# Half of the states of a selective scan form their input on ScalarE and TensorE, and the sum over states is made of transposes

## The chip, the cores and the metric

The kernel runs on one core of a Trainium2 chip. The metric is the device time of one execution in microseconds (us), the median of a few runs. Five engines work at once, each through its own queue in order: TensorE (PE, with its weight loads as PEld), VectorE (DVE), ScalarE (ACT), GpSimd (POOL) and SyncE (SP, which here only issues DMAs).

## The reference

Two layers are computed. The change touches the first, a two-dimensional selective scan over a (4, 48, 48, 128) input. Each image is normalised, projected to 256 channels, convolved with a depthwise 3x3 filter and passed through SiLU. The 48x48 positions are then read in four orders (by rows, by columns, and both backwards), and in each order a recurrence with 16 states per channel runs over all 2304 positions:

```
def step(h, inp):
    dt_l, u_l, B_l, C_l = inp
    dA = jnp.exp(dt_l[..., None] * A)
    h = h * dA + (dt_l * u_l)[..., None] * B_l[:, :, None, :]
    y = jnp.einsum('bkdn,bkn->bkd', h, C_l)
```

B and C are one number per position and state, dt and u one per position and channel, A one per channel and state. The four results are added, with the term D*u, then normalised over the channels, gated with a SiLU branch and projected to 128 channels. The second layer, a spectral attention block, is the same before and after the change.

## The kernel before

Channels lie on the 128 partitions, in two halves (NF = 2), and positions along the free axis. An image's direction is cut into chunks of 480, 480, 480, 480 and 384 positions. The order of the work is written out by hand: for each image, direction and chunk, the 16 states are 16 *steps*, 1280 in all. `advance` puts a new step into a window of ten and runs the stages of the table `LAGS` on the steps in it, each stage a fixed number of steps behind:

- `fetch`: SP reads the rows of C for two states from DRAM, spread over all partitions (`cbc`); for every fourth state also the row of B (`bbc`).
- `spread`: for the other states TensorE makes the row of B on all partitions, a bf16 matmul with the selecting matrix `pick`, into the one PSUM buffer `pb`.
- `drive_in`: VectorE multiplies `du` (dt*u) with that row into `db`, 128x960; `drive_pool` does it on GpSimd for every fourth state, from `bbc`.
- `decay`: ScalarE makes exp(dt*A) for the two halves in `da`, one of two PSUM buffers, and copies the value carried from the chunk before into the element of `db` between the halves.
- `scan`: VectorE runs the recurrence h = da*h + db over both halves in one instruction. Between the halves da is 0, so that the second half starts from its own carried value.
- `read_out`: GpSimd multiplies h with the row of C (`hc`). `carry_on`: ScalarE copies the last value of each half into `carry`.
- `sum_up`: TensorE adds `hc` to the PSUM accumulators `yp` by a matmul with the identity, one per half. The first step of a chunk also adds D*u or the sum of the earlier directions (`y`).
- `put_away`: after the last state ScalarE copies `yp` out, into `y`, or in the last direction into `yb`, from which the generator `back` finishes the chunk.

At the end of each `advance`, `piece` takes one piece of the side work that waits in `later`: generators that project the next direction (`project`, `project_chunk`), prepare the next image (`front`) or finish chunks (`back`). They use the PSUM bank `pp`. `drive` makes `du` for the next chunk on GpSimd. All engine instructions but the DMAs are kept in the order in which they are written; nearly all bear the line number of that wrapper (L50), so that the profile's groups are told apart by the tiles' names.

Of the kernel before, what the change touches and what calls it, by code (L numbers as in the profile page):

```python
# [21 lines left out]
L = T * H  # L22
D = 256
NF = D // 128
N = 16
# [6 lines left out]
LC = 480  # L32
CHUNKS = [(s, min(LC, L - s)) for s in range(0, L, LC)]
# [20 lines left out]
def first_layer(ctx, tc, io, x1_dram, sp_dram, d_w, d_m):  # L54
# [16 lines left out]
    ring = ctx.enter_context(tc.tile_pool(name="l0_ring", bufs=7))  # L71
# [3 lines left out]
    ps_y = ctx.enter_context(tc.tile_pool(name="l0_psy", bufs=1, space=PSUM))  # L75
    dram = ctx.enter_context(tc.tile_pool(name="l0_dram", bufs=8, space=DRAM))
# [25 lines left out]
    w_x = const.tile([128, K, NF, R + 2 * N], F32, name="w_x")  # L102
# [6 lines left out]
    p3 = const.tile([NX, N], F32, name="p3")  # L109
# [63 lines left out]
    def open_up(b, x, made):  # L173
# [3 lines left out]
        st = small.tile([128, 6, 6], F32, tag="st", name=f"st{b}")  # L177
# [180 lines left out]

    def load_dt(b, k):
        w_dt = two.tile([32 + R, D], F32, tag="w_dt", name=f"w_dt{b}_{k}")  # L360
        nc.sync.dma_start(w_dt[32 : 32 + R], io["dt_proj_wT"][k])
        return w_dt

    def project_chunk(c, w_dt, xc):
# [10 lines left out]
        xd = two.tile([32 + R, LC], F32, tag="xd", name=f"xd{c.t}")  # L375
# [12 lines left out]
        for f in range(NF):  # L388
            pd = side(f"pd{c.t}_{f}")
            on.tensor.matmul(  # L390
                pd[:, 0:n],
                w_dt[32 : 32 + R, f * 128 : (f + 1) * 128],
                xd[32 : 32 + R, 0:n],
                start=True,
                stop=True,
            )
            yield
            on.scalar.activation(c.dt[:, f, 0:n], pd[:, 0:n], AF.Identity, bias=b_dt[:, k, f : f + 1])

# [74 lines left out]
    NQ = 2  # L474

    das = [ps_a.tile([128, 2 * BANK], F32, name=f"da{j}") for j in range(2)]
    for da in das:
        on.vector.memset(da[:, BANK - 1 : BANK], 0.0)  # L480
    carries = [const.tile([128, N, NF], F32, name=f"carry{j}") for j in range(2)]

    def halves(ap, n):

        return ap[:, 0 : 2 * (n + 1)].rearrange("p (f n) -> p f n", f=NF)[:, :, 0:n]
# [10 lines left out]
    class Step:  # L496


        def __init__(self, c, i):
            self.c, self.i = c, i  # L500

    def fetch(u):
        c, i, n = u.c, u.i, u.c.n
        if i % NQ == 0:
            c.cbc = three.tile([128, NQ, LC], F32, tag="cbc", name=f"cbc{c.t}_{i}")
            nc.sync.dma_start(c.cbc[:, :, 0:n], c.cd[N + i : N + i + NQ, 0:n].partition_broadcast(128))
        u.cbc = c.cbc[:, i % NQ : i % NQ + 1, 0:n]
        if i % 4 == POOLS:
            u.bbc = two.tile([128, 1, LC], F32, tag="bbc", name=f"bbc{c.t}_{i}")
            nc.sync.dma_start(u.bbc[:, :, 0:n], c.cd[i : i + 1, 0:n].partition_broadcast(128))  # L510

    def drive_pool(u):

        c, i, n = u.c, u.i, u.c.n
        u.db = three.tile([128, NF * (LC + 1)], F32, tag="db", name=f"db{c.t}_{i}")
        if i % 4 == POOLS:
            on.gpsimd.tensor_mul(halves(u.db, n), c.du[:, :, 0:n], u.bbc[:, :, 0:n].to_broadcast([128, NF, n]))

    def spread(u):
# [4 lines left out]
        if i % 4 == POOLS:  # L524
# [4 lines left out]
        )  # L529

    def drive_in(u):
        c, i, n = u.c, u.i, u.c.n
        if i % 4 != POOLS:
# [4 lines left out]
    def decay(u):  # L538
        c, i, n = u.c, u.i, u.c.n
        u.da = das[i % 2]  # L540
        for f in range(NF):
            q = c.k * NF + f
            o = BANK if f else BANK - 1 - n
            on.scalar.activation(u.da[:, o : o + n], c.dt[:, f, 0:n], AF.Exp, scale=a_neg[:, q, i : i + 1])
        on.scalar.copy(u.db[:, n : n + 1], c.carry[:, i, 1 - c.rev : 2 - c.rev])

    def scan(u):
        c, i, n = u.c, u.i, u.c.n
        u.h = four.tile([128, NF * (LC + 1)], F32, tag="h", name=f"h{c.t}_{i}")
        m = 2 * n + 1  # L550
        ha, aa, ba = u.h[:, 0:m], u.da[:, BANK - 1 - n : BANK + n], u.db[:, 0:m]
# [4 lines left out]
    def read_out(u):  # L556
        c, i, n = u.c, u.i, u.c.n
        u.hc = four.tile([128, NF, LC], F32, tag="hc", name=f"hc{c.t}_{i}")
        on.gpsimd.tensor_mul(u.hc[:, :, 0:n], halves(u.h, n), u.cbc.to_broadcast([128, NF, n]))

    def carry_on(u):
        c = u.c
        if not c.final:
            on.scalar.copy(c.carry[:, u.i], halves(u.h, c.n)[:, :, 0 if c.rev else c.n - 1])

    def sum_up(u):

        c, i, n = u.c, u.i, u.c.n
        if i == 0:
            c.yp = [ps_y.tile([128, 512], F32, tag=f"yp{f}", name=f"yp{c.t}_{f}") for f in range(NF)]  # L570
            for f in range(NF):
                if c.k == 0:
                    on.tensor.matmul(
                        c.yp[f][:, 0:n], ddiag[:, f], c.im["xc"][:, f, c.s : c.s + n], start=True, stop=False
                    )
                else:
                    yv = at(c.im["y"], c.k, c.s, n)[:, f]
                    on.tensor.matmul(like(c.yp[f][:, 0:n], c.k), ident, yv, start=True, stop=False)
        for f in range(NF):
            on.tensor.matmul(c.yp[f][:, 0:n], ident, u.hc[:, f, 0:n], start=False, stop=(i == N - 1))  # L580

    def put_away(u):
# [4 lines left out]
        if c.k == ORDER[-1]:  # L587
            while len(backs) > 1:
                drain(backs.popleft())
            yb = two.tile([128, NF, LC], F32, tag="yb", name=f"yb{c.t}")  # L590
            for f in range(NF):
                on.scalar.copy(yb[:, f, 0:n], c.yp[f][:, 0:n])
            backs.append(back(c.b, c.s, n, yb, c.im["x"], c.im["w"], c.im["wb"]))
            later.append(backs[-1])
        else:
            if "y" not in c.im:
# [1390 lines left out]
```

## Time and profile before

| | us |
|---|---|
| median of 3 runs | 4990.82 |
| lowest and highest | 4985.44, 4992.6 |
| the profiled execution, span | 4987.4 |
| first scan begins, last scan ends | 76.8, 4178.2 |

The profiled execution is known by its span alone: no time of its own was taken outside it. The median of the runs, which are other executions, is 3.4 us above it. In the lines of the profile, a group of instructions is told by line, engine, operation, output<-inputs, shapes and count; then its busy time in us and the mean of one in ns; then the idle time of the engine just before it and what ended that. An f32 matmul is recorded as two, each with its weight load; a transpose as one. "128*96 128x128" on a matmul means weights of 128x96 and a moving operand of 128x128.

### The profile page before, as it was taken

Reading aid. Unit: us, or ns where it says so; the run is one execution under the profiler, and the core shown is the slowest. Engines: PE = TensorE matmul, PEld = TensorE weight load, DVE = VectorE, ACT = ScalarE, POOL = GpSimd, SP = SyncE. Lnnn points to the kernel's source line nnn. Section 1 sums busy time; section 2 is a strip of 40 time slices with the busy share of each in tenths; the row PEclk is TensorE's granted clock in tenths of the full one; section 3 lists DMA queues with packets and bytes.
Section 4 is the critical chain, followed back from the end, with each engine's and each line's share of the span. In section 5 each row is a group of like instructions: output and inputs, shape, how many; then the busy total and the mean of one; then the engine's idle time right before and its main releaser. Section 6 shows DMA issues by size and latency. Waiting matters only on the chain.

```text
span 4987.4 us, 44228 instructions
## 1 busy us (share of the span) xinstructions
PE 4176.6 (84%) x12444; PEld 1913.7 (38%) x12444; DVE 4169.9 (84%) x2901; ACT 2964.0 (59%) x6608; POOL 3992.7 (80%) x2188
## 2 busy tenths in 40 slices
PE   6888898888798998887989888877888786879876
PEld 3334433333343333333433333333333432445443
DVE  3599998989899989898999998888999985557636
ACT  3566566666666666766666676665767654323344
POOL 4589998989899989888999998888999985146631
PEclk9989999999899999998999999998999988989977
DMA  1223232323232333232323233233333322236636
GB/s 55 74 87 100 94 113 91 104 85 102 90 107 94 116 95 99 89 100 92 104 95 115 93 98 94 98 104 92 104 107 102 105 92 90 48 71 147 146 101 151
DMA packets 276388, 491.57 MB, mean 99 GB/s; under 512 B 105685, under 2 KB 189781, under 8 KB 275565
## 3 DMA queue, kind: packets, MB, share of 16 engines
q1 hardware_dynamic: 270560, 485.67, 32.5%
q10 hardware_dynamic: 5580, 3.08, 0.3%
q8 instruction: 98, 1.61, 0.1%
q14 instruction: 150, 1.22, 0.1%
HBM read 453.49 MB, written 35.38 MB: 98 GB/s over the span
## 4 chain that ended last, share of the span: by engine, by line
DVE 18%; PE 15%; issue 7%; ACT 7%; POOL 3%; DMA 2%; SPq 1%; DVEq 0%; POOLq 0%; ACTq 0%
DVE h L50 12%; PE yp L50 4%; ACT da L50 3%; DVE db L50 3%; PE acc L1404 2%; ACT L50 1%; PE sc L1267 1%; POOL v L1400 1%; POOL db L50 1%; PE pi_p L50 1%; DMA xrep<-dxt 1%; ACT dt L50 1%; POOL hc L50 1%; ACT ws L50 1%; PE px L50 1%
## 5 line engine op out<-in xcount | busy, mean ns | idle before, releaser
L50 POOL TENSOR_TENSOR hc<-h,cbc 128x960 f32<-128x960 f32 (+1 forms) x1280 | 2718.7, 2140 | 448.3 <-DVE h L50 335.8
L50 DVE TENSOR_TENSOR_SCAN h<-da,carry,db 128x961 f32<-128x961 f32 (+1 forms) x1280 | 2701.8, 2129 | 164.9 <-ACT carry L50 107.1
L50 ACT ACTIVATE da<-dt,a_neg 128x480 f32<-128x480 f32 (+1 forms) x2560 | 1666.6, 651 | 1176.6 <-DVE h L50 1130.8
L50 PE MATMUL yp<-hc,ident 128*128 128x480 f32 (+1 forms) x5120 | 2277.5, 572 | 17.7 <-POOL hc L50 17.4
L50 PEld LDWEIGHTS yp<-hc,ident 128*128 128x128 f32 x5120 | 1005.6, 198 | 1381.0 <-issue 1006.0
L50 DVE TENSOR_TENSOR db<-du,pb 128x960 f32<-128x960 f32 (+1 forms) x960 | 1063.8, 1108 | 233.2 <-PE pb L50 177.8
L50 POOL TENSOR_TENSOR db<-du,bbc 128x960 f32<-128x960 f32 (+1 forms) x320 | 688.9, 2153 | 17.2 <-DMA d_m<-in_wK 8.5
L50 PE MATMUL pb<-bs,pick 112*128 112x480 bf16 (+1 forms) x960 | 358.0, 373 | 351.9 <-DVE db L50 350.0
L50 PE MATMUL pc<-pad,cdiag 128*128 128x480 f32 (+1 forms) x630 | 284.1, 563 | 6.6 <-ACT pad L50 6.6
L1400 POOL TENSOR_TENSOR v<-grep,xrep 128x768 f32<-128x768 f32 x96 | 174.9, 1823 | 87.3 <-PE acc L1404 48.7
L50 ACT COPY db<-carry 128x1 f32<-128x1 f32 x1280 | 228.5, 178 | 19.5 <-POOL db L50 13.5
L1404 PE MATMUL acc<-v,attn_c 128*64 128x384 f32 x1152 | 211.5, 504 | 26.7 <-DVE v L1396 13.6
L50 POOL TENSOR_TENSOR du<-dt,xc 128x480 f32<-128x480 f32 (+1 forms) x160 | 204.9, 1281 | 34.0 <-ACT dt L50 34.0
L1396 DVE TENSOR_TENSOR v<-gp,xrep 128x1536 f32<-128x1536 f32 x96 | 168.0, 1756 | 74.4 <-PE acc L1404 46.4
L50 PE MATMUL px<-xc,w_xp 128*112 128x480 f32 (+1 forms) x320 | 214.0, 756 | 17.1 <-ACT xc L50 13.3
L50 PEld LDWEIGHTS <-pick 112*128 112x128 bf16 x960 | 97.7, 102 | 329.4 <-issue 306.1
L50 ACT ACT_TABLE_LOAD x148 | 189.9, 1283 | 50.3 <-DMA ws_M<-in_wM1s 26.7
L50 PE MATMUL pd<-xd,w_dt 8*128 8x480 f32 (+1 forms) x320 | 168.0, 605 | 40.0 <-ACT bs L50 24.5
L50 ACT COPY carry<-h 128x2 f32<-128x2 f32 x1024 | 194.4, 190 | 0.0
L50 PEld LDWEIGHTS pc<-pad,cdiag 128*128 128x128 f32 x630 | 122.1, 194 | 139.4 <-issue 114.6
L50 PE MATMUL yp<-y,ident 128*128 128x480 f32 (+1 forms) x240 | 166.3, 823 | 0.2
L1404 PEld LDWEIGHTS acc<-v,attn_c 128*64 128x64 f32 x1152 | 119.2, 139 | 108.5 <-issue 53.7
(366 smaller groups left out, 3102.2 us busy)
## 6 DMA issues: line engine op xcount, KB each, us to landing
cbc<-cd SPq DMA_DIRECT2D x512, 480.0 KB
bbc<-cd SPq DMA_DIRECT2D x256, 240.0 KB
cbc<-cd SPq DMA_DIRECT2D x128, 384.0 KB
xrep<-dxt SPq DMA_DIRECT2D x48, 576.0 KB
bbc<-cd SPq DMA_DIRECT2D x64, 192.0 KB
grep<-dgt SPq DMA_DIRECT2D x16, 576.0 KB
x<-in_xT SPq DMA_DIRECT2D x16, 288.0 KB
xr<-in_xT SPq DMA_DIRECT2D x16, 288.0 KB
```

The lines of the kernel that those rows point to most:

```text
L50: return lambda *args, **kw: self._tc.keep_in_program_order(emit(*args, **kw))
L1267: nc.tensor.matmul(sc[64 * b : 64 * b + 64, g, 0 : 8 * T], qs[:, j, n, 2 * pair + b], f[b][:, 8 * g : 8 * g + 8], start=(jn == 0), stop=False,
L1396: nc.vector.tensor_mul(v, gp[:, None, :, 0:NC].to_broadcast([128, 2, 2, NC]), x[:, :, 0:2])
L1400: nc.gpsimd.tensor_mul(v3, r[:, 2:3].to_broadcast([128, 2, NC]), x[:, :, 2])
L1404: nc.tensor.matmul(acc[c][64 * b : 64 * b + 64, 0:NC], attn_c[:, 2 * pair + b, g, q], v[:, b, c] if c < 2 else v3[:, b], start=first, stop ...
```

## The change

States with an even number keep the way through `pb` and VectorE; none is made on GpSimd any more. States with an odd number go another way. For each chunk `turn_du` transposes `du` on TensorE, so that positions lie on partitions, in blocks of 128 (`blocks`), and ScalarE copies it out of PSUM; `project_chunk` does the same for B (`bt`). Then B is one number per partition, and `scale` multiplies with it on ScalarE, four activations of 128x256 with a scale by partition. `turn` transposes the result back on TensorE, eight blocks, straight into a PSUM buffer of its own (`das[1]`), with the carried value put between the halves by a matmul with the identity. The scan of an odd state reads du*B from there and its decay from one of two SBUF buffers (`decays`); that of an even state reads its decay from `das[0]` and du*B from `db` in SBUF. The gap between the halves is two elements wide.

`sum_up` transposes `hc` into the accumulators, eight blocks for each state, positions on partitions; `put_away` copies them out, and the new generator `gather` transposes them back and adds D*u or the earlier sum. Copies of carried values move from ScalarE to GpSimd. C is fetched one row at a time into five buffers. The window is nine steps long; odd steps take one piece more (`extra`); ring and buffer counts change with the room in SBUF.

```
+    def turn_du(c):
...
+        for h in range(0, 4, 2):
+            some = [(q, r) for q, r in blocks(n) if h <= q < h + 2]
+            p = side(f"pdu{c.t}_{h}")
+            for q, r in some:
+                for f in range(NF):
+                    o = (q - h) * 256 + f * 128
+                    on.tensor.transpose(p[0:r, o : o + 128], c.du[:, f, q * LB : q * LB + r], ident)
+            yield
...
+                on.scalar.copy(c.dut[0:r, q : q + m], p[0:r, o : o + m * 256].rearrange("p (q d) -> p q d", d=256))
...
     das = [ps_a.tile([128, 2 * BANK], F32, name=f"da{j}") for j in range(2)]
-    for da in das:
-        on.vector.memset(da[:, BANK - 1 : BANK], 0.0)
+    on.vector.memset(das[0][:, BANK - GAP : BANK], 0.0)
+    decays = [const.tile([128, 2 * LC + GAP], F32, name=f"decay{j}") for j in range(2)]
...
     def fetch(u):
...
+        u.cbc = rows.tile([128, 1, LC], F32, tag="cbc", name=f"cbc{c.t}_{i}")
+        nc.sync.dma_start(u.cbc[:, :, 0:n], c.cd[N + i : N + i + 1, 0:n].partition_broadcast(128))
...
     def spread(u):
...
+        if u.turned:
             return
...
+        u.db = two.tile([128, NF * (LC + GAP)], F32, tag="db", name=f"db{c.t}_{i}")
+        on.gpsimd.tensor_copy(u.db[:, n : n + GAP], before(u))
...
+    def scale(u):
...
+        drain(c.turn)
+        u.scaled = two.tile([LB, 4, NF * 128], F32, tag="scaled", name=f"scaled{c.t}_{i}")
+        for q, r in blocks(n):
+            on.scalar.activation(u.scaled[0:r, q], c.dut[0:r, q], AF.Copy, scale=c.bt[0:r, q, i : i + 1])
+
+    def turn(u):
...
+        for f in range(NF):
+            o = BANK if f else BANK - GAP - n
+            for q, r in blocks(n):
+                on.tensor.transpose(
+                    das[1][:, o + q * LB : o + q * LB + r], u.scaled[0:r, q, f * 128 : (f + 1) * 128], ident[0:r, 0:r]
+                )
+        on.tensor.matmul(das[1][:, BANK - GAP : BANK], ident, before(u), start=True, stop=True)
...
+        da, o = (decays[i // 2 % 2], LC) if turned else (das[0], BANK - GAP)
...
+        ba = das[1][:, BANK - GAP - n : BANK + n] if u.turned else u.db[:, 0 : 2 * n + GAP]
...
     def carry_on(u):
         c = u.c
         if not c.final:
-            on.scalar.copy(c.carry[:, u.i], halves(u.h, c.n)[:, :, 0 if c.rev else c.n - 1])
+            on.gpsimd.tensor_copy(c.carry[:, u.i], halves(u.h, c.n)[:, :, 0 if c.rev else c.n - 1])
...
     def sum_up(u):
...
+        for q, r in blocks(n):
             for f in range(NF):
...
+                o = q % 2 * 256 + f * 128
+                on.tensor.matmul(
+                    c.yp[q // 2][0:r, o : o + 128],
+                    u.hc[:, f, q * LB : q * LB + r],
+                    ident,
+                    start=(i == 0 and q % 2 == 0 and f == 0),
+                    stop=(i == N - 1),
+                    is_transpose=True,
+                    skip_group_check=True,
+                )
+
+    def gather(c, yt):
...
+            for q, r in blocks(n):
+                on.tensor.matmul(
+                    p[:, q * LB : q * LB + r],
+                    yt[0:r, q, f * 128 : (f + 1) * 128],
+                    ident[0:r, 0:r],
+                    start=(q == 0),
+                    stop=False,
+                    is_transpose=True,
+                    skip_group_check=True,
+                )
...
+            on.tensor.matmul(like(p[:, 0:n], k), w, v, start=False, stop=True, skip_group_check=True)
...
+    def extra(u):
+        if u.turned:
+            piece()
...
     LAGS = (
-        (0, fetch), (9, put_away), (2, drive_pool), (4, drive_in), (5, scan), (4, decay), (6, carry_on),
-        (5, read_out), (3, spread), (8, sum_up),
+        (3, fetch), (8, put_away), (4, drive_in), (5, scan), (4, decay_here), (4, turn), (3, decay_there),
+        (2, extra), (2, scale), (3, spread), (5, read_out), (5, carry_on), (7, sum_up),
     )
-    window = deque([None] * 10, 10)
+    window = deque([None] * 9, 9)
```

Further, `drive` for the next chunk is called at the states 6 and 10 (9 and 12 before a new direction) instead of 11 and 14, with `turn_du` queued after the second; `RING` is 6 instead of 7; and `w_dt`, `xd` and `st` have one buffer instead of two.

## The prediction

> **What bounds the kernel now.** I read the page's busy line first, then its costliest groups, then the busy time in stretches, then who VectorE waits for.
>
> ```profile
> PE 4176.6 (84%) x12444; PEld 1913.7 (38%) x12444; DVE 4169.9 (84%) x2901; ACT 2964.0 (59%) x6608; POOL 3992.7 (80%) x2188
> ...
> L50 POOL TENSOR_TENSOR hc<-h,cbc 128x960 f32<-128x960 f32 (+1 forms) x1280 | 2718.7, 2140 | 448.3 <-DVE h L50 335.8
> L50 DVE TENSOR_TENSOR_SCAN h<-da,carry,db 128x961 f32<-128x961 f32 (+1 forms) x1280 | 2701.8, 2129 | 164.9 <-ACT carry L50 107.1
> L50 ACT ACTIVATE da<-dt,a_neg 128x480 f32<-128x480 f32 (+1 forms) x2560 | 1666.6, 651 | 1176.6 <-DVE h L50 1130.8
> L50 PE MATMUL yp<-hc,ident 128*128 128x480 f32 (+1 forms) x5120 | 2277.5, 572 | 17.7 <-POOL hc L50 17.4
> ...
> L50 DVE TENSOR_TENSOR db<-du,pb 128x960 f32<-128x960 f32 (+1 forms) x960 | 1063.8, 1108 | 233.2 <-PE pb L50 177.8
> L50 POOL TENSOR_TENSOR db<-du,bbc 128x960 f32<-128x960 f32 (+1 forms) x320 | 688.9, 2153 | 17.2 <-DMA d_m<-in_wK 8.5
> ...
> L50 ACT COPY db<-carry 128x1 f32<-128x1 f32 x1280 | 228.5, 178 | 19.5 <-POOL db L50 13.5
> ...
> L50 ACT COPY carry<-h 128x2 f32<-128x2 f32 x1024 | 194.4, 190 | 0.0
> ```
>
> All 1280 steps (4 images, 4 directions, 5 chunks, 16 states) have one scan each; the first begins at 76.8 us and the last ends at 4178.2 us, so a step takes 3.20 us. The next view gives busy time of a quiet stretch (32 full steps), of one where finished chunks also go through `back` (48 steps), and of the whole scan stage.
>
> ```profile
> core 0: us, PE busy (x) PEld busy (x) DVE busy (x) ACT busy (x) POOL busy (x), PEclk, DMA share, GB/s
> 2464.00:2561.00 97.00, 89.71 (x221) 38.51 (x221) 94.98 (x58) 59.09 (x147) 91.91 (x45) 1.00 0.31 103
> 1991.00:2164.00 173.00, 142.32 (x321) 58.39 (x321) 148.59 (x93) 117.49 (x237) 144.68 (x70) 0.95 0.29 89
> 76.80:4178.20 4101.40, 3490.27 (x8494) 1533.77 (x8493) 3711.77 (x2341) 2657.15 (x6075) 3647.89 (x1856) 0.95 0.31 97
> ```
>
> In the quiet stretch VectorE is busy 98% of the time and GpSimd 95%: a step is 3.03 us, VectorE 2.97, GpSimd 2.87, ScalarE 1.85. In the `back` stretch a step is 3.60 us with VectorE at 3.10 and ScalarE at 2.45: nobody is full. Over the stage VectorE has 2.90 us of work a step, GpSimd 2.85, ScalarE 2.08. So **VectorE bounds, GpSimd is a hair behind, and 0.3 us a step go to waits**. Which ones, from 600 to 3900 us:
>
> ```profile
> DVE h L50 <- ACT carry L50: 80.9, 24, 4.8
> DVE db L50 <- PE pb L50: 64.5, 73, 3.0
> DVE h L50 <- ACT db L50: 28.0, 8, 8.3
> ```
>
> Few but long waits for ScalarE: bursts (five Softplus between two table loads, 7.0 us together) during which no decay is made; and many short ones for the row of B that TensorE spreads.
>
> [...] For 96 elements with a pointer scale [...] the trace's two such copies span 0.64 us, a pitch of 0.28. [...] 27 transposes and small neighbours between 4296.3 and 4302.3 us ran at a granted clock of 0.50, and the clock then rose to 1.00 and stayed there through a long run of transposes. [...] The new scans keep one operand in PSUM (even states the decay, odd ones du*B), as now; no run here has the other case.
>
> **The change, part by part** (per step, chunk of 480; one chunk in five has 384, where the per-element share is 0.8 of it).
>
> VectorE. The multiply into `db` falls from 3 states in 4 to 2 in 4. Its start-to-start time is 1.07 us (1108 mean less overlap), so 0.25 x 1.07 = 0.27, 0.26 on the mix. 2.90 becomes **2.64**. Scans get one element more: 0.002 us.
>
> GpSimd. The multiply for every fourth state goes: 688.9/1280 = 0.54. New are the two-element carry copies (0.8 a step) and the gap copy (0.5 a step). The nearest row is GpSimd's copy of a few f32 columns, 28 in 3.9 us, 0.14 each: 0.18. 2.85 becomes **2.50**. Both carry copies stand behind the `hc` multiply that waits for the same scan, so they add work but no new wait; if each cost twice that, 2.68, still covered by ScalarE.
>
> ScalarE. Gone: the two carry copies, 0.22. New on odd states: four activations of 256 elements with a pointer scale. From the measured pitch, 0.28 + 160 x 0.84 = 0.41; four are 1.65, 0.79 a step on the mix. Bounds 0.36 and 0.50 each. New per chunk: copies of the turned du and of the turned sum out of PSUM (one of 512 and two of 256 each, 0.48 and 0.26 by the pitch of 0.45 at 480), two small ones: 2.2 us, 0.14 a step. The odd exponentials write SBUF: without the wait of 33 ns that the first of a pair now has they save about 0.05; I count that. 2.08 - 0.22 + 0.79 + 0.14 - 0.05 gives **2.74**, and 2.9 with the upper price of the scaling. ScalarE becomes as full as VectorE: 2.51 against 2.70 in the quiet stretch, 3.12 against 2.83 in the `back` stretch.
>
> TensorE. The sum over states now takes four records per state at 0.40 us pitch, 1.61. A transposed block is one record:
>
> ```profile
> 4317.24 1.51 PE L1164 MATMUL pxn<-ident,xa 128*96 128x128 f32 x12
> ```
>
> Twelve in 1.51 us, the last one's 0.27 included: pitch 0.11. Eight are 0.9. Odd states add eight more and a two-column matmul with a full weight load in two records (0.22): 0.55 a step. B rows fall from 0.15 to 0.1. The turning of du and B and the gathering, 20 transposes a chunk: 0.14. Together 1.76 becomes **1.69**: no gain, no loss. At half clock all of it doubles.
>
> Queues. SP issues 1280 row fetches instead of 960 transfers, 0.32 us each: 0.1 ms of a queue that waited 2884 us for `hc` alone. 73.7 MB of B rows are no longer read, and the DMA engines stand at 31%; nothing waits for them. I cost this at nothing: five row buffers keep fetches ahead; without that cover `read_out` would wait for landings.
>
> **New waits.** (1) `turn` on TensorE must wait until the previous odd scan has read the one PSUM buffer. Behind it in TensorE's queue stand a side piece, the B row of the next even state, and the sum. After that scan VectorE has one scan (2.11) before the multiply that needs the B row; TensorE needs 1.1 for the turn, 0.2 and a latency of 0.16 for the row, so the piece may take 0.6 us. A piece is nothing, or one or two f32 matmuls (0.8 to 1.6). With half of them at 0.8 to 1.0: 0.1 to 0.2 a pair, **0.08 a step**, about what the B row costs now. (2) The even decay waits for the previous even scan, with 3.2 us until its own: a slack of 1.8, as now. The odd decay has two SBUF buffers and more room.
>
> **Sum.** Quiet: 2.70 + 0.08 + 0.05 of gaps = 2.83, from 3.03. `back`: ScalarE 3.12 and about 8% of its time lost to TensorE's pieces, 3.4 from 3.60. A Softplus burst still stops VectorE some 4 us and ScalarE then catches up more slowly. I take 0.13 a step for 1200 steps, 156 us; the first direction (80 steps), where TensorE's convolution sets the pace, gains nothing; an extra turn at the start and a gather at the end cost 5. The profiled execution is 4987 - 151 = 4836 us of span; the median of the runs stands 3.4 above that span, so **4840 us**.
>
> **Rivals.** *VectorE stays the bound everywhere*, the more room of the odd decays swallowing the bursts: 2.64 + 0.2 = 2.84 a step, 1200 x 0.31 = 370 less, 4620. Against it: ScalarE's 3.12 in the `back` stretches. Chance 0.10. *TensorE's queue behind the turn* (slower): should the piece before the B row be 1.6 us on the average, VectorE waits 1.0 a pair, 0.5 a step. Against the 0.26 saved, and with some 0.12 of the present `pb` and burst waits falling inside it, 0.12 a step is lost: 1280 x 0.12 = 150 more, 5140. It decides from pieces of about 1.1 us. For it: convolution pieces are two matmuls; against it: many pieces hold no matmul. Chance 0.21. *ScalarE in order*: scaling at 0.50 each gives 2.9 a step, and if it idles 12% on TensorE and table loads, 3.3: 5110. Chance 0.13. *Gain eaten exactly*: 0.06. *The change doesn't do what it says*: if the transposes hold the clock at half, TensorE's 1.69 and about 0.7 of other matmuls double to 4.8 a step, near 7000 us; 0.02. The likeliest, VectorE and ScalarE sharing the bound at about 3.02 a step, has 0.48 and a range of its own of 4750 to 4950.
>
> **Numbers.** A measurement of this kernel tells 0.2%, 10 us, from no change. Faster 0.48 + 0.10 = 0.58; same 0.06; slower 0.36. The range leaves out half of the first rival's case and the far end of the slower ones: 4660 to 5130.
>
> **What would show it.** `db<-du,pb` x640; scans still near 2.13; scaled copies near 0.45 long at 0.41 pitch; ScalarE's share of the stage from 65% to about 89%; TensorE's clock 0.9 or more. I am wrong on the covers if VectorE's wait for `pb` goes above 0.2 us a step, and on ScalarE if scans wait for the even decay outside bursts.

## The result: 8% slower, and VectorE waits for the row of B

The median after is 5390.91 us (four runs, 5388.78 to 5400.38), beside 4990.68 before: a ratio of 1.0807, 95% interval 1.0792 to 1.0822. That is 400 us slower. The profiled execution has a span of 5398.6 us. The first scan begins at 80.7 us (76.8 before) and the last ends at 4575.3 (4178.2 before), so a step takes 3.51 us instead of 3.20.

The busy line and the costliest groups of the changed kernel, in the columns that the prediction's fences have:

```profile
PE 4388.2 (81%) x24396; PEld 3060.2 (57%) x24396; DVE 3831.3 (71%) x2580; ACT 3784.5 (70%) x7327; POOL 3356.8 (62%) x3534
...
L54 POOL TENSOR_TENSOR hc<-h,cbc 128x960 f32<-128x960 f32 (+1 forms) x1280 | 2543.3, 1987 | 1415.2 <-DVE h L54 1027.6
L54 DVE TENSOR_TENSOR_SCAN h<-da,carry,db 128x962 f32<-128x962 f32 (+1 forms) x640 | 1356.1, 2119 | 246.5 <-ACT da L54 228.1
L54 PE MATMUL yp<-ident,hc 128*128 128x128 f32 (+1 forms) x9728 | 1446.6, 302 | 15.8 <-POOL hc L54 15.3
L54 DVE TENSOR_TENSOR_SCAN h<-decay,carry,da 128x962 f32<-128x962 f32 (+1 forms) x640 | 1364.0, 2131 | 0.0
...
L54 DVE TENSOR_TENSOR db<-du,pb 128x960 f32<-128x960 f32 (+1 forms) x640 | 711.2, 1111 | 822.9 <-PE pb L54 787.7
L54 ACT ACTIVATE scaled<-turned,bt 128x256 f32<-128x256 f32 (+1 forms) x2432 | 1035.9, 497 | 1.7
```

The work moved as the diff says. The scans last what they lasted (2.12 and 2.13 us). There are 640 multiplies into `db` instead of 960. Odd scans (`decay`) wait for nothing that the profile shows. Read the last number of the `db` line: those 640 multiplies stood 822.9 us, 787.7 of them for TensorE's row of B; before, 960 of them stood 233.2. One line now holds more waiting than the kernel lost. (Of each of the two sums, one long wait lies ahead of the first scan, where the kernel starts: 54.4 us here, 46.5 before. Inside the scan stage VectorE waits 733 us for the row instead of 128. Nearly all kernels below have such a first wait in their figure, of 46 to 56 us.)

Busy time in the scan stage, which answers to the prediction's third row (after the span: PE, PEld, DVE, ACT, POOL, then clock, DMA share and GB/s):

```profile
core 0: us, PE busy (x) PEld busy (x) DVE busy (x) ACT busy (x) POOL busy (x), PEclk, DMA share, GB/s
80.70:4575.30 4494.60, 3702.74 (x20428) 2679.97 (x20426) 3375.57 (x2021) 3474.21 (x6783) 3012.75 (x3199) 0.87 0.26 72
```

By 1280 steps: VectorE 2.64 us, ScalarE 2.71, GpSimd 2.35, in steps of 3.51. No engine is full; before, VectorE and GpSimd nearly were. VectorE's gaps of over 60 ns between the first and the last scan, added up from the trace, went from 389 to 1118 us. Who waits for whom in the changed kernel (us in total, times, longest; "..." stands for lines left out):

```profile
DVE db L54 <- PE pb L54: 787.7, 426, 54.4
...
PE da L54 <- DVE h L54: 266.1, 208, 3.8
DVE h L54 <- ACT da L54: 228.1, 52, 26.6
...
ACT y L54 <- PE pg L54: 155.1, 90, 4.3
...
ACT xd L54 <- PE px L54: 140.1, 66, 5.1
...
ACT xc L54 <- PE pc L54: 121.0, 40, 10.0
...
ACT dt L54 <- PE pd L54: 101.8, 94, 3.6
```

The second line is the turn of an odd state that waits, at the head of TensorE's queue, for the scan that still reads the one PSUM buffer. The last four are ScalarE at side work: it waits for TensorE to fill a PSUM bank, in the scan stage always `pp`. That is 518 us in these four tiles, 496 of them inside the stage. Before, the three of them that existed cost 150, 120 of them inside the stage:

```profile
ACT xc L50 <- PE pc L50: 72.5, 19, 10.5
ACT dt L50 <- PE pd L50: 39.5, 34, 4.4
ACT xd L50 <- PE px L50: 38.0, 24, 3.6
```

### The profile page after: what moved, and what is told of

It reads as the page before. It is cut to its first block, busy times and chain, and to the rows that moved or that the text cites. A ratio compares the mean times of both kernels' runs of the same rounds, so it can differ in the third digit from the quotient of the medians.

```text
span 5398.6 us, 70142 instructions
## 1 busy us (share of the span) xinstructions
PE 4388.2 (81%) x24396; PEld 3060.2 (57%) x24396; DVE 3831.3 (71%) x2580; ACT 3784.5 (70%) x7327; POOL 3356.8 (62%) x3534
## 5 line engine op out<-in xcount | busy, mean ns | idle before, releaser
L54 POOL TENSOR_TENSOR hc<-h,cbc 128x960 f32<-128x960 f32 (+1 forms) x1280 | 2543.3, 1987 | 1415.2 <-DVE h L54 1027.6
L54 DVE TENSOR_TENSOR_SCAN h<-da,carry,db 128x962 f32<-128x962 f32 (+1 forms) x640 | 1356.1, 2119 | 246.5 <-ACT da L54 228.1
L54 PEld LDWEIGHTS yp<-ident,hc 128*128 128x128 f32 (+1 forms) x9728 | 1291.2, 154 | 422.5 <-issue 269.8
L54 PE MATMUL yp<-ident,hc 128*128 128x128 f32 (+1 forms) x9728 | 1446.6, 302 | 15.8 <-POOL hc L54 15.3
L54 DVE TENSOR_TENSOR_SCAN h<-decay,carry,da 128x962 f32<-128x962 f32 (+1 forms) x640 | 1364.0, 2131 | 0.0
L54 DVE TENSOR_TENSOR db<-du,pb 128x960 f32<-128x960 f32 (+1 forms) x640 | 711.2, 1111 | 822.9 <-PE pb L54 787.7
L54 ACT ACTIVATE scaled<-turned,bt 128x256 f32<-128x256 f32 (+1 forms) x2432 | 1035.9, 497 | 1.7
L54 PEld LDWEIGHTS da<-ident,scaled 128*128 128x128 f32 (+1 forms) x4864 | 603.7, 155 | 699.8 <-DVE h L54 215.0
L54 ACT ACTIVATE da<-dt,a_neg 128x480 f32<-128x480 f32 (+1 forms) x1280 | 828.7, 647 | 239.5 <-DVE h L54 217.9
L54 PE MATMUL da<-ident,scaled 128*128 128x128 f32 (+1 forms) x4864 | 720.9, 296 | 316.3 <-DVE h L54 266.1
L54 ACT ACTIVATE decay<-dt,a_neg 128x480 f32<-128x480 f32 (+1 forms) x1280 | 790.6, 665 | 0.4
```

What stands on the lines that cost most here:

```text
L54: return lambda *args, **kw: self._tc.keep_in_program_order(emit(*args, **kw))
```

## The experiments

All ratios are to the kernel before, measured beside it. Theory A is the prediction's second rival: TensorE's queue behind the turn. Its rivals: ScalarE's added load, the transposed sum with TensorE's slower clock, and the side work.

### The order of TensorE's queue

Three orders of the table `LAGS`. `row_first` puts the row of B ahead of turn and side piece; `extra_last` only moves the odd step's second piece to the end; `both_order` does both.

```
-        (3, fetch), (8, put_away), (4, drive_in), (5, scan), (4, decay_here), (4, turn), (3, decay_there),
-        (2, extra), (2, scale), (3, spread), (5, read_out), ...
+        (3, fetch), (8, put_away), (4, drive_in), (5, scan), (3, spread), (4, decay_here), (4, turn), (3, decay_there),
+        (2, extra), (2, scale), (5, read_out), ...
```

> The changed kernel with one line moved: the row of B for the next even state (spread) is issued before the turn and the extra piece of the same round. Queue theory: VectorE's 788 us of waits for pb come from the row standing behind a turn that waits for the odd scan, and behind a piece; they fall below 250 us, and about half of what is saved comes back as waits of the scans: 5390 - 300 = 5090. Piece theory: the chains of side pieces through one PSUM bank hold TensorE and ScalarE as long as before, VectorE waits for the decay or the turn instead: 5300 to 5390. Clock theory (TensorE simply has more work at 0.87 of its clock): 5350 to 5390.

Measured: 5293.33 us, 1.0607 [1.0585, 1.0629], 98 us off the changed kernel. VectorE's waits in this kernel:

```profile
DVE h L54 <- ACT da L54: 466.9, 217, 28.8
DVE db L54 <- PE pb L54: 326.4, 168, 53.8
```

The wait for the row lost 461 us, the kernel 98. Half of what was won (239 us) is back one line higher: the even scan, which comes next, waits for its decay from ScalarE. So theory A's mechanism is there, but the time is 200 us above what it wanted and close to the piece theory's range: taking the wait for the row away uncovers a second one of nearly its size.

```
-        (2, extra), (2, scale), (3, spread), (5, read_out), (5, carry_on), (7, sum_up),
+        (2, scale), (3, spread), (5, read_out), (5, carry_on), (7, sum_up), (2, extra),
```

> The changed kernel with the extra piece of odd steps moved behind the row of B and the sum. Queue theory: the piece is half of what stands before the row: pb waits 400 us, time 5200. Piece theory: the same pieces at another place, 5300 to 5400. Clock theory: 5380.

Measured: 5522.39 us, 1.1062 [1.1044, 1.1081]: 131 us worse, and above all three theories. The wait for the row falls to 599.6 us, but that for ScalarE's decay rises to 467.6.

> Both moves: the row first, the extra piece last. Queue theory: about 5050, little better than the row first alone. Piece theory: within 60 us of the changed kernel, 5330 to 5400. Clock theory: 5380.

Measured: 5499.26 us, 1.1013 [1.0997, 1.103], again above all three. The row costs 297.1 us, the decay 654.2. Where the pieces stand in the order is worth more than 100 us, and the total follows neither wait alone.

### The load on ScalarE and TensorE

`scale_one` scales only the first of the blocks (the rest of the product is left out, every turn reads the first); `turn_one` turns back only the first block per half, the others in PSUM staying zero.

```
-        for q, r in blocks(n):
+        for q, r in blocks(n)[0:1]:
             on.scalar.activation(u.scaled[0:r, q], c.dut[0:r, q], AF.Copy, scale=c.bt[0:r, q, i : i + 1])
```

> The changed kernel with three of the four scaling activations of an odd state left out (all blocks are turned back from the first one, so du*B is not computed for most positions); TensorE, VectorE and GpSimd do what they did. ScalarE theory: ScalarE has 2.68 us of work a step and 0.4 us of waits for TensorE's side pieces, so it sets the pace; with 0.6 us a step less it does not: 5390 - 400 or more, under 5000. TensorE-queue theory (the row behind turn and piece): ScalarE is not the cause, 5300 to 5390. Clock theory: 5390.

Measured: 5265.31 us, 1.0554 [1.0538, 1.057]: 126 us less. 1792 of 2432 activations are gone, and ScalarE's busy time in the scan stage falls from 3474 to 2775 us. Less than a fifth of these 699 us reaches the time, and the row still costs 695.2 us. The kernel is neither under 5000, as the ScalarE theory had it, nor quite in the range of the other.

```
-            for q, r in blocks(n):
+            for q, r in blocks(n)[0:1]:
                 on.tensor.transpose(
```

> The changed kernel with six of the eight transposes of an odd state left out (only the first block of each half is turned back, the rest of the scan's input stays zero): TensorE has 0.33 us a step less, ScalarE what it had. ScalarE theory: 5250 to 5390, for TensorE's pieces come a little earlier. TensorE-queue theory: the row comes 0.7 us earlier in each pair, half of the pb waits are gone, 5000 to 5100.

Measured: 5270.93 us, 1.0571 [1.0549, 1.0592]: 120 us less, with 632.1 us of waiting for the row, not half of 788. Neither load by itself is the bound.

`all_three` joins both to `row_first`.

> Row first, three of four scaling activations and six of eight turning transposes left out (du*B is not computed for most positions), all side work kept. Alone they won 98, 125 and 120 us. If the loss is the fullness of TensorE and ScalarE together, the gains add up or more: 4950 to 5050. If the hand-overs of the side work remain whatever the load: 5100 to 5200.

Measured: 5097.39 us, 1.0222 [1.0199, 1.0245], 294 us less than the changed kernel; the three single gains add to 343. Fullness as the cause would have had them add up or more; 5097 is 3 us below the range of the other theory. Its busy time from 80 to 4400 us:

```profile
80.00:4400.00 4320.00, 3480.35 (x17063) 2369.15 (x17063) 3398.16 (x2104) 2804.96 (x5032) 3026.80 (x3280) 0.83 0.28 77
```

ScalarE has 2805 us of work here, 65% of the stretch, the share it had before the change, and VectorE and GpSimd have less than before. The kernel is still 109 us slower than the one before. The load of the added instructions cannot be the whole cause.

### Copies moved to VectorE

`copies_vector` is `row_first` with the three copies that serve the turned tiles (`dut`, `bt` and the turned sum) on VectorE, which has room.

```
-            on.scalar.copy(c.bt[0:r, q : q + m], ...)
+            on.vector.tensor_copy(c.bt[0:r, q : q + m], ...)
```

> The kernel with the row first, and the copies of turned du, turned B and the turned sum out of PSUM moved from ScalarE to VectorE (0.13 us a step). ScalarE theory: VectorE's 467 us of waits for the even decay fall by about 150, time 5290 - 100 to 150. TensorE-queue theory: VectorE gets more work and nothing is won, 5290 to 5400.

Measured: 5414.23 us (5378.71 to 5441.81), 1.0848 [1.0799, 1.0898], worse than `row_first` by 121. VectorE's waits:

```profile
DVE h L54 <- ACT da L54: 220.4, 110, 7.5
DVE bt L54 <- PE pt L54: 155.4, 33, 27.4
DVE turned L54 <- PE yp L54: 142.5, 79, 8.2
```

The scans' wait for ScalarE fell from 466.9 to 220.4 us, so the copies on ScalarE were part of it. But a copy at the end of a chain through TensorE held whichever queue it stood in, and now that is the queue of the scans (155.4 us ahead of `bt` and 142.5 ahead of `turned`). Room in busy time is not room for a wait.

### The transposed sum and TensorE's clock

`sum_identity` is the changed kernel with the old sum (f32 matmuls with the identity, no gather).

```
-        for q, r in blocks(n):
-            for f in range(NF):
...
+        for f in range(NF):
+            on.tensor.matmul(c.yp[f][:, 0:n], ident, u.hc[:, f, 0:n], start=False, stop=(i == N - 1))
```

> The changed kernel with the sum over states as before: identity matmuls into yp, no turned sum, no gather. Queue theory: TensorE has 0.7 us a step more in a queue that is late already: 5500 to 5700. Piece theory: the gathers (46 of the 220 long VectorE gaps have a gather alone in TensorE's queue, 144 us) are gone and win 150 us or more, less the longer sums: 5250 to 5400. Clock theory: TensorE at 3.5 us a step: 5700.

Measured: 5357.32 us, 1.0735 [1.0719, 1.0751]: 34 us better, at a granted clock of 0.945 instead of 0.867. VectorE waits as long for the row as in the changed kernel (803.9 us). `sum_id_row` puts the row first in it as well.

> The changed kernel with the sum by identity matmuls and the row issued first. It combines two edits that won 34 and 98 us alone. If TensorE's queue order and its clock are the causes they add up or better, for at 0.945 of the clock what is left are pb waits of 800 us: 5100 to 5200. If the load of TensorE and ScalarE waiting for each other is what remains, 5250 to 5300.

Measured: 5336.48 us, 1.0689 [1.0671, 1.0707], worse than both expectations. From 80 to 4400 us GpSimd now waits long for the sum to give back `hc`:

```profile
POOL hc L54 <- PE yp L54: 716.2, 359, 8.1
```

`before_tsum` is the reverse: the kernel before with the transposed sum and its gather, for which `hc` has three buffers instead of four and two small tiles one instead of two.

> The kernel before with one part of the change alone: the sum over states by accumulating transposes and the gather, all else (inputs, carries, order) as it was; hc has three buffers and two small tiles one, for room. By the terms of the prediction TensorE has 0.7 us a step less, ScalarE 0.07 more. If the transposed sum itself is the harm (gathers chained through one bank): 5050 to 5150. If the harm needs a full ScalarE: 4930 to 5000.

Measured: 5146.09 us, 1.0318 [1.0301, 1.0336], clock 0.81, in the range for gathers chained through one bank. But the run doesn't price the sum alone: with three buffers GpSimd waits for TensorE's sum, which it had hardly done (26.2 us in the whole kernel before):

```profile
POOL hc L51 <- PE yp L51: 225.9, 184, 15.1
```

Is it the clock? In the records of the stage, leaving out the first chunk, TensorE stood 403 us at half clock before and 1123 after; a scan came every 4.74 us of half clock after, every 3.17 us of full clock. But the clock fell after stretches in which TensorE had little to do (after, it was occupied for 0.42 of the 3.41 us before a fall, the median; the last section has the other figures), so that a low clock can follow from late work as well as cause it. Two runs bear on this. In `sum_identity` TensorE stands at half clock for 266 us, counted alike, less than in the kernel before; it is still 366 us slower, with the wait for the row there in full. Half clock is thus not needed for the loss, though that kernel gives TensorE a longer sum.

`tsum_fill` adds to `before_tsum` four bf16 matmuls of 384 columns with zero weights in 14 of the 16 states, which keep TensorE occupied and add nothing to the sum.

```
+        for _ in range(FILL if 0 < i < N - 1 else 0):
+            on.tensor.matmul(c.yp[0][:, 0:384], nought, ones, start=False, stop=False, skip_group_check=True)
```

> The kernel before with the transposed sum alone, plus four bf16 matmuls of 384 columns with zero weights added to the accumulators in each step (0.64 us of TensorE work a step at full clock, nothing changed in the result). Clock theory, new form: the transposed sum made TensorE so light that windows with little work come often, the granted clock falls to half for 1649 us instead of 403, and the late half-clock work is the whole loss; with the filler the half-clock time falls under 700 us and the time from 5146 to 5000 or less, although TensorE does more. Work theory: more work in TensorE's queue costs time, 5200 to 5300. Gather theory (the chained gathers are the loss): 5140 to 5200.

Measured: 5155.33 us, 1.0329 [1.0314, 1.0345]. From 80 to 4400 us, `before_tsum` first, `tsum_fill` second:

```profile
80.00:4400.00 4320.00, 3205.24 (x13810) 2071.93 (x13809) 3731.82 (x2380) 2747.12 (x6317) 3669.26 (x1937) 0.80 0.30 94
```

```profile
80.00:4400.00 4320.00, 3532.10 (x18267) 2257.28 (x18266) 3727.97 (x2375) 2739.07 (x6311) 3675.27 (x1937) 0.92 0.29 94
```

The clock rose from 0.80 to 0.92, the time at half clock fell from 1649 to 642 us, and VectorE got through no more work (3731.82 and 3727.97 us). The expectation of the clock theory, 5000 or less, did not come true, and the time lies in the range of the gather theory: whatever the higher clock wins in this kernel, it is no more than the filler's own place in the queue costs. `row_fill` does a like thing to `row_first`, four bf16 matmuls into `pb` ahead of each row:

```
+        w = ps_b.tile([128, 512], F32, tag="pb", name=f"fill{u.c.t}_{u.i}")
+        for _ in range(FILL):
+            on.tensor.matmul(w[:, 0 : u.c.n], pick[:, 0:1].to_broadcast([NX, 128]), u.c.bs[:, 0 : u.c.n], ...)
```

> The kernel with the row first, plus four bf16 matmuls of 480 columns ahead of the row in each pair of steps (0.8 us a pair at full clock), where TensorE waits for a scan anyway. Clock theory: half-clock time from 1000 to under 600 us, time from 5293 to 5150 to 5220. Work theory: 5320 to 5450.

Measured: 5502.72 us, 1.105 [1.0993, 1.1108], clock 0.911 instead of 0.873, and the wait for the row 601.2 us instead of 326.4. That is worse than either theory had it. Half-clock time fell from 1000 to 659 us only. The fill stands in front of the row and cost more than the higher clock returned; this run speaks for the queue, not on the clock.

### Without the side work

Three kernels leave out the projections of directions 2 to 16 and the preparation of images 2 to 4 (later directions reuse the first one's dt, B and C): `before_bare`, `after_bare` and, with the row first, `row_bare`.

```
         for c in chunks:
+            d = [o for o in directions[0] if o.s == c.s][0]
+            c.dt, c.bs, c.cd = d.dt, d.bs, d.cd
...
+        return
```

> The kernel before without its side work after the first direction: the projections of directions 2 to 16 and the preparation of images 2 to 4 are left out (their steps reuse the first direction's dt, B and C and the first image's convolution), so dt, B, C and xc are not computed there; back, put_away and everything in the steps stay. A base for the next two. VectorE and GpSimd near full: 1200 steps at 2.95 instead of 3.15: 4700 to 4780.

> The changed kernel with the same side work left out (the projections and preparations above; the turning of du and the gather stay). Side-work theory (TensorE and ScalarE hand each piece to and fro in order, both near full, so that each one's wait becomes the other's and VectorE's): without the pieces the steps run near VectorE's 2.64: 4350 to 4600, below the kernel before without its side work. Step theory (the turn, the row and the sum in the step itself lose the time): it stays slower than that one by 200 us or more.

> The kernel with the row first, with the same side work left out. Side-work theory: the order of the row matters little once the pieces are gone, within 60 us of the changed kernel so treated. Step theory: 100 us or more faster than it, as with the side work.

Measured:

| | with side work | without | side work costs |
|---|---|---|---|
| before | 4990.7 | 4870.59 (0.9769 [0.9752, 0.9785]) | 120 |
| after | 5390.9 | 4881.14 (0.9789 [0.9775, 0.9804]) | 510 |
| after, row first | 5293.3 | 4730.64 (0.9483 [0.9468, 0.9498]) | 563 |

Without side work the changed kernel stands 11 us from the one before instead of 400; with the row first it is 140 us *faster*. Neither theory had this right. The side-work theory wanted 4350 to 4600 for `after_bare`, and the step theory 200 us more than `before_bare` (which itself missed its 4700 to 4780).

VectorE's gaps, counted as in the section on the result, tell how the loss divides. They are 270 us in `before_bare`, 634 in `after_bare` and 487 in `row_bare`, against 389 and 1118 with side work. So the steps of the changed kernel make VectorE wait 364 us longer even when they are alone, and this eats the 356 us by which its own work has become shorter. Of the 729 us of gaps that the change adds, half are in the steps and half come with the side work.

Of the two waits of VectorE, in `after_bare` and in `row_bare`:

```profile
DVE db L54 <- PE pb L54: 441.7, 212, 54.3
```

```profile
DVE h L54 <- ACT da L54: 142.3, 88, 24.2
DVE db L54 <- PE pb L54: 129.2, 34, 53.8
```

The queue's order costs 151 us even here: on this the step theory (100 or more) was right, and the side-work theory (within 60) wrong. On the other hand the decay's 466.9 us of `row_first` are 142.3 without side work. So the change gains where the steps are alone and the row is first, and loses where they share ScalarE and TensorE with the projections.

### Where the side work bites

`piece` keeps to a generator until it yields FREE or WAIT. `project_chunk` yields neither: a projection can be left only between two chunks, where the next one must wait for a buffer of the ring. `turning`, called at state 10 of a chunk, drains the `gather` of the chunk before, and must first push the projection of the chunk that is under way to its end: all of it, then the whole gather, at one place of the order. This is such a place in the changed kernel (start and duration in us, then engine, line, operation and tiles; in brackets the idle time before it and what ended that; lines of weight loads, of GpSimd and SyncE, and of other work of TensorE are left out):

```profile
1925.40 2.21 DVE L54 TENSOR_TENSOR_SCAN h<-decay,carry,da 128x962 f32<-128x962 f32 x1
1926.20 0.66 ACT L54 ACTIVATE dt<-pd,b_dt 128x480 f32<-128x480 f32 x1 [1.19 <-PE pd L54]
1926.91 0.40 PE L54 MATMUL pt<-ident,xd 16*128 16x16 f32 x4 [0.75 <-ACT dt L54]
1927.35 0.27 ACT L54 COPY bt<-pt 128x48 f32<-128x48 f32 x2 [0.49 <-PE pt L54]
1927.67 0.63 PE L54 MATMUL pg<-ident,turned 128*128 128x128 f32 x4 [0.36 <-ACT bt L54]
1928.14 1.78 PE L54 MATMUL pg<-y,ident 128*128 128x480 f32 x2
1929.96 0.96 ACT L54 COPY y<-pg 128x480 f32<-128x480 f32 x1 [2.34 <-PE pg L54]
1930.97 1.06 PE L54 MATMUL pg<-ident,turned 128*128 128x128 f32 x4 [1.05 <-ACT y L54]
1931.82 1.86 PE L54 MATMUL pg<-y,ident 128*128 128x480 f32 x2
1933.72 0.98 ACT L54 COPY y<-pg 128x480 f32<-128x480 f32 x1 [2.80 <-PE pg L54]
1934.50 1.36 ACT L54 ACTIVATE da<-dt,a_neg 128x480 f32<-128x480 f32 x2
1935.94 2.22 DVE L54 TENSOR_TENSOR_SCAN h<-da,carry,db 128x962 f32<-128x962 f32 x1 [8.33 <-ACT da L54]
```

TensorE and ScalarE take turns through the one bank `pp`, each stopping while the other works, and the decay of the next even state stands behind the last copy. VectorE is idle for 8.33 us. `row_free` is `row_first` with two kinds of place where `project_chunk` may be left:

```
             on.scalar.copy(c.bs[rows, 0:n], px[rows, 0:n])
+        if c.number >= len(CHUNKS):
+            yield FREE
...
             on.scalar.activation(c.dt[:, f, 0:n], pd[:, 0:n], AF.Identity, bias=b_dt[:, k, f : f + 1])
+            if c.number >= len(CHUNKS):
+                yield FREE
```

> The kernel with the row first, and project_chunk lets other side work in at three points (after bs, and after each half of dt), so that the gather of a finished chunk no longer stands behind a whole projection and is not forced through in one burst with it when the next du is turned. VectorE's idle time before the scans of states 5 and 6, where that burst falls, is 286 us in 15 directions with the row first and 107 before. Burst theory: it falls under 160, time 5293 - 100 to 150. Hand-over theory (each TensorE-ScalarE-TensorE hand-over of a piece costs, wherever it stands): the waits only move to other states, 5260 to 5330.

Measured: 5097.39 us, 1.0215 [1.0198, 1.0232]: two insertions that remove no instruction take 196 us from `row_first`. Its longest waits are these:

```profile
POOL hc L54 <- DVE h L54: 552.5, 393, 14.8
...
DVE h L54 <- ACT da L54: 364.9, 185, 24.3
DVE db L54 <- PE pb L54: 208.2, 92, 52.6
```

Both of VectorE's fell by more than 100 us, and ScalarE's wait for the gather (`y<-pg`) went from 147 to 64 us. The idle time of VectorE ahead of the scans of states 5 and 6, the first that are written after that place, added up from the trace over directions 2 to 16: 98 us before the change (the expectation has 107), 249 after, 287 in `row_first`, 196 in `row_free`. Without the last chunk of each direction, in which the next direction's projection is itself waited for, `row_first` has 201 and `row_free` 56. I had expected under 160 in all; the missing part is in those last chunks. The 91 us won at this place are half of the gain. Some 37 us more come from the first direction (398 us in `row_first`, 361 in `row_free`), in which the projection of the second one runs; the rest is spread over other states. Whether the same stops would help the kernel before was not run; leaving out its side work altogether gains 120 us there, less than the 196.

`row_free_late` also makes `du` later in the first direction (at states 11 and 14, as before).

> The one before with du made at states 11 and 14 in the first direction, as in the kernel before, instead of 6 and 10. There the next chunk's front work must be ready by then and is forced through; the first direction took 397 us in the changed kernel and 320 before. If that forcing is the cause: 40 to 77 us less than row_free. If the first direction is slow for TensorE's convolutions anyway: within 15 us of it.

Measured: 5104.61 us, 1.0231 [1.0216, 1.0246], no better. The earlier `drive` is not what costs the first direction.

### A version that was to beat both

`quarter` starts from `sum_id_row` and sends only every fourth state the new way, with three `db` buffers and one `scaled`. The states 1, 5, 9 and 13 take their decay from `das[1]`, where ScalarE first clears the gap between the halves.

```
-            self.c, self.i, self.turned = c, i, i % 2 == 1
+            self.c, self.i, self.turned = c, i, i % 4 == 3
```

> An attempt at a better kernel: as the one before (sum by identity matmuls), but every fourth state goes the new way through ScalarE and TensorE instead of GpSimd's multiply, and carries are copied on GpSimd. VectorE 2.90 us a step as before, GpSimd 2.35 instead of 2.85, ScalarE about 2.4, TensorE 0.3 more than before. If GpSimd's fullness is part of the loss before: 4900 to 4980. If TensorE and ScalarE waiting for each other decides: 5050 to 5200.

Measured: 5416.85 us, 1.0855 [1.0836, 1.0873], slower than either expectation and than `sum_id_row`. GpSimd's wait for `hc` is again long (457.7 us from 80 to 4400 us), as in `sum_id_row`; three instead of four buffers of `hc` under the slower identity sum are suspected, but no run isolates them. No version run here that does the whole work beats the kernel before.

## Why the prediction was wrong

**The work was right.** VectorE 2.64 us a step (2.64 forecast), ScalarE 2.71 (2.74), GpSimd 2.35 (2.50; the `hc` multiply fell from 2140 to 1987 ns, which is the difference). The scaled copies take 0.43 each, busy (0.41, counted with 0.84 ns an element; in the kernel before, from 600 to 3900 us, exponentials of 480 and 384 elements lasted 667 and 587 ns on the mean, 0.83 an element). In the sum, at full clock, a transpose has a pitch of 0.11, as read before, and at half clock one of 0.21. ScalarE's share of the stage is 77% and not 89% because the stage became longer, not because the work is less. TensorE's 1.69 can't be read off directly, because more of it ran at half clock: 2.89 us busy a step, 2.73 before.

**The step that failed is "New waits", and with it the "Sum" that was built on it.** The wait for the row was put at 0.08 a step, "about what the B row costs now". Inside the scan stage it was 0.57, against 0.10 before. The warning mark of 0.2 was passed almost threefold. Two errors are in that number. First, only the turn and one free piece were put ahead of the row. In the 768 us that VectorE stood idle ahead of these multiplies inside the stage, 733 of them for the row, TensorE was executing the turn for 208 us, the row itself for 121 and the sum for 48; the pieces of projection, gather and convolution took most of the rest. Second, pieces were priced as matmuls of 0.8 to 1.6 us. But TensorE's queue also stops where a piece needs its bank back from ScalarE (`px` waited 140.6 us for ScalarE's copy `bs`), which now had less time to spare. Before, ScalarE was idle 1.1 us of a step; after, 0.8, of which the waits above are half.

**The second rival was half right.** It named the mechanism (the row behind turn and piece) and the side (slower), at 150 us. `row_first` prices it: 98 us with side work, 151 without. What the rival, like every other case, left out is the rest: side work that cost 120 us and now costs 510. The "Sum" carries 0.13 a step over to all but the first direction, with nothing for this.

**"About 8% of ScalarE's time lost to TensorE's pieces"** was too small and had the wrong place. In the four tiles shown above ScalarE lost 496 us inside the scan stage, 11% of the whole of it, not 8% in the `back` stretches; and part of the loss comes in bursts, as VectorE's 8.33 us show. What `turning` drains is nowhere in the prediction: the new gather was costed at 20 transposes and some copies, 0.14 us a step on TensorE and as much on ScalarE, and not as a place where a whole projection is forced through. With the row first, giving the projection places to stop gave back 196 us.

**"The first direction gains nothing"**: it lost 77 us (320.6 to 397.2). **"5 us" at start and end** were 4 and 14. The other fifteen directions lost 317.

**A gain is there, under two conditions.** Between `before_bare` and `row_bare` lie 140 us, 0.11 a step; the prediction had 156. But `row_bare` has neither the order of the changed kernel nor its side work, so that the two numbers come near each other partly by luck: without the side work alone (`after_bare`) nothing is gained. The error was to add up busy shares and carry the sum to steps whose waits had grown. Both engines that receive the work, ScalarE and TensorE, are those that the side work alternates between.

**The other rivals.** *VectorE stays the bound everywhere*: it is busy 75% of the stage. *ScalarE in order* foretold 5110 from a dearer scaling and 12% of idle time: the scaling was not dearer, and with 699 us of ScalarE's work taken away the kernel gains 126. *Half clock* wasn't total, as expected, but half-clock time rose from 403 to 1123 us. `tsum_fill` shows that less of it need not help, and `sum_identity` loses 366 us with less half clock than the kernel before; in the changed kernel itself, with its lighter sum, the share of the clock was not separated.

**What stays open.** `row_free` is 104 us slower than before. The first direction (361 us against 320), the last chunks of the directions and more half clock are in it; no run divides them. The shorter window, the three buffers of `hc` and the carry copies on GpSimd were not tried one by one. Nor is it settled why the old sum, with the row first, holds `hc` so long.

## What to carry to other kernels

Before moving work to an engine with free time, ask what that free time does now: if side work hands a buffer to and fro between that engine and another, its free time may be what makes each hand-over prompt (here ScalarE's fell from 1.1 to 0.8 us a step, and the cost of the side work rose from 120 to 510 us). Price a new consumer at a point in a hand-ordered queue by everything that must be forced through ahead of it, not by its own instructions, and give long generators places to stop. To see whether a lost gain is there at all, run both kernels without the side work: here that showed how much of the loss is in the steps and how much comes with the pieces, which removing single instructions had not.

## What the runs showed of the hardware

The granted clock fell in pieces of 3.41 us: in the records of the changed kernel's scan stage, 160 dips that make up the 1123 us, each a multiple of it to within 0.1% of a piece. In the 3.41 us before a dip TensorE was not idle throughout: it was occupied for 0.42 of that time (median; 0.31 in the kernel before), and in 51 of the 160 cases for more than half. In the 3.41 us before a rise it was occupied all the time (median), and never for less than 0.83 of it (0.78 before). So a queue that runs and stops in turns stood at half clock for a quarter of the stage, at a busy share of 82%. At half clock TensorE's work took about twice as long, as the prediction counted: a transpose of the sum had a pitch of 0.21 us instead of 0.11, and in the kernel before an f32 matmul of the sum one of 0.80 instead of 0.40 (medians). Nothing was seen to set transposes apart, as the prediction had read in the trace of the kernel before: the changed kernel, whose sum is made of them, spent three quarters of the stage at full clock (a granted clock of 0.87 over the stage).

A pair of exponentials of 480 elements took 1.36 us into PSUM, as in the fence above (`da`, x2), and 1.27 into SBUF (`decay`; both are medians of 512 pairs of the changed kernel). So moving the odd decays to SBUF did save what was counted for it, 0.05 a step.
